# GpSimd in place of ScalarE for the column added onto routed token rows, with a shorter fill in the scatter step

## Chip, cores and metric

One Trainium2 chip, one of its cores. The metric is the device time in microseconds (us) of one execution, and its median over three runs. Engines are named as in the profile: PE (TensorE matmul), PEld (its weight loads), DVE (VectorE), ACT (ScalarE), POOL (GpSimd) and SP (SyncE, which here only starts DMAs).

## What is computed

An input of 32 images, each 128 channels by 56 x 56 pixels, in float32, runs through two layers:

```python
# layer 0
x = x + conv3x3(sign(groupnorm(x)), sign(w)) * Alpha
# layer 1, on tokens: t is (32, 3136, 128)
t = t + q * sum_n(k * v)                  # q, k, v from layernorm(t)
n = layernorm(t)
p = softmax(n @ router_w + router_b)      # 8 experts, the best two per token
top_p, top_i = top_k(p, 2); top_p /= sum(top_p)
t = t + sum_k top_p[k] * (n @ expert_w[top_i[k]] + expert_b[top_i[k]])
```

The last line is the part around the change: each of 3136 tokens per image goes to two of eight experts, and the two results, weighted, are added to the token.

## The kernel before

An image has 25 chunks of tokens, 24 of 128 rows and one of 64; a chunk in SBUF is a tile of 128 partitions (tokens) by 136 columns: 128 channels and 8 columns for the routing. The experts are computed in two ways. For the first chunks of each image, and for all chunks of the last four images, they are **dense**: all eight experts run on every token, and the gates multiply the input (`gated`, L1172, on DVE, then eight expert products on PE, L1190). For the other chunks the tokens are **sorted**. Images 0 to 27 form four groups (8, 8, 7 and 5 images) in which 8, 8, 8 and 12 chunks are dense, so 17 (or 13) chunks per image are sorted, 456 in all. A sorted chunk takes this way:

1. `row_scalars` (DVE, L1371 to L1390) works out per token a column `a` (a layernorm shift) and four scalars, which it writes into columns 128 to 131 of the token's row. `row_numbers` (DVE, L1350 to L1355) works out to which row of a DRAM table `rows` each token goes, by its pair of experts.
2. `row_add` (ACT, L1395) adds `a` onto the 128 channels of the chunk, in place: one activation of 128 x 128 float32 with a bias per partition.
3. `scatter` (POOL, L1402) is an indirect DMA that writes the chunk's 128 rows of 132 columns to their places in `rows`. POOL's share of that work is the profile's DMA_INDIRECT.
4. When all images of a group are scattered, tiles of 128 rows of one pair of experts are loaded from `rows` (`tile_load`, SP), turned (PE, L1735; ACT, L1746), multiplied with the two experts' weights (PE, L1758), scaled and shifted (ACT, L1776 and L1783), summed (DVE, L1788 and L1793) and stored to a DRAM table `res`.
5. `gather` (POOL, L1481), again an indirect DMA, fetches the rows of `res` for a chunk, again 456 in all. They are turned back to channels (`back_turn`, PE, L1501), copied (ACT, L1514) and stored to the output.

Each indirect DMA, scatter or gather, passes through `in_turn` (L1579 to L1587): it waits until the fourth indirect DMA before it has landed, and after it POOL runs a **fill**, a memset of an unused tile `idle` (128 partitions x 480 bytes, L1586), before the next one. The scatter has a `nop` ahead of its DMA.

The order of instructions on every engine is set by a planner, `in_order`, that runs when the kernel is built. Every piece of work is a step with a due time, an engine, an estimated duration and the steps that it waits for (`after`). Rings such as `ROOM["sent"] = 4` limit how far one step may run ahead of another in the plan. Each engine then issues its steps strictly in that order. An image's work is due 60 us after that of the image before, and about three images are in flight (`HELD = 3` buffers of tokens), so that the transposes of image i+3 into the token buffer (`xt`, PE, L677) wait for the scatters of image i. The scatter steps are planned at `SEND = 1.75` us, and so are the gathers; `row_scalars` of image i waits for the last `row_add` of image i-2, since the column `a` has two buffers. For images 0 to 7 POOL also sums one-hot blocks (`hot_blocks`, L1305 and L1307, three adds of 128 x 112 bfloat16), whose result goes by way of PE's `places` and ACT's `count_on` to `row_numbers`.

Of the kernel before, what the change touches and what calls it, by code (L numbers as in the profile page):

```python
# [48 lines left out]
AF = mybir.ActivationFunctionType  # L49
ALU = mybir.AluOpType  # L50
# [4 lines left out]
C = 128  # L55
# [22 lines left out]
}  # L78
ON_POOL = 8
IN_FLIGHT = 4  # L80
SEND = 1.75
HELD, LOADS, LOAD_LANDS = 3, 4, 10.0

GATE_LANDS, SPREAD_LANDS, STORE_LANDS, TILE_LANDS, GATHER_LANDS = 5.0, 6.5, 5.0, 6.0, 12.0
# [3 lines left out]
Q_GROUP = 3  # L88
# [11 lines left out]
BANKS, EMPTIES = ("ps", "acc", "ff"), 7.0  # L100
ROOM = dict(
    ps=5, acc=1, ff=2, y=3, qs=3, tt=4, bc=4, gt=2, gated=2,
    t_in=3, turned=2, v=3, w=2, back=12, sent=4, o=2, late=3,
)


# [82 lines left out]
def conv_attn_moe_kernel(  # L189
# [19 lines left out]
    nc = tc.nc  # L209
# [3 lines left out]
    n_ck = -(-n_tok // C)  # L213

    def rows_of(c):
        return min(C, n_tok - c * C)
# [21 lines left out]
    const = ctx.enter_context(tc.tile_pool(name="const", bufs=1))  # L238
# [241 lines left out]
    def at(due, key, engine, work, do, *args, after=(), take=(), free=(), delay=0.0, slack=0.0):  # L480


        if isinstance(work, float):
            steps[key] = Step(due, key, engine, work, do, args, after, take, free, delay, slack, 0.0)
            return
        running = []

        def go_on():
            if not running:
                running.append(do(*args))  # L490
            next(running[0], None)

        lag = LAG if isinstance(work, list) else 0.0
        for j, w in enumerate(work):
            last = j == len(work) - 1
            part = key if last else (*key, "part", j)
            steps[part] = Step(
                due, part, engine, w, go_on, (), [(*key, "part", j - 1)] if j else after,
                [] if j else take, free if last else [], delay if last else 0.0, slack, lag,
            )  # L500
# [53 lines left out]
    def plan_image(i: int):  # L554
        s = base(i)
        d = {"x": x_all[i % HELD], "tok": tok_all[i % HELD]}
        st1, st2 = st1_all[i % 2], st2_all[i % 2]
        move = move_all[i % 2]
        n_dense = DENSE[group_of[i]] if i in group_of else n_ck
# [56 lines left out]
        for k in range(n_load):  # L616
# [3 lines left out]
                after=[("load", i, k - 1) if k else ("load", i - 1, 1)]  # L620
                + ([("gn_sum", 0, GN_PARTS - 1)] if i == 1 else [])
                + reads_to((k + 1) * n_tok // n_load),
                delay=7.0 if i == 1 else 13.0 if i < HELD else LOAD_LANDS,
            )
        for j in range(GN_PARTS):
# [6 lines left out]
                after=[("gn_neg", i), ("conv", i - 1, min(j + 1, n_conv - 1))],  # L632
# [3 lines left out]
            after=[("gn_sum", i, j) for j in range(GN_PARTS)],  # L636
# [4 lines left out]
            after=[("gn_mean", i), ("gn_sign", i - 2, GN_PARTS - 1)], free=[("ps", ("gn_mean", i))],  # L641
# [64 lines left out]
        for b in range(n_conv):  # L706
            at(
                s + 5.5 * b, ("conv", i, b), "PE", 1.75, conv, b,
                after=[("gn_sign", i, j) for j in range(min(b + 2, GN_PARTS))]
                + [("conv", i, b - 1) if b else ("conv", i - 1, n_conv - 1), ("binary", 2)],  # L710
                take=["ps"],
# [3 lines left out]
                after=[("conv", i, b)], free=[("ps", ("conv", i, b))],  # L715
            )
        for g in range(n_blk):
# [5 lines left out]
                after=[("conv_add", i, b), ("xt", i, g - 1)] + sent_from(i - HELD, g),  # L723
                take=["ps"],
# [3 lines left out]
                after=[("xt", i, g)], free=[("ps", ("xt", i, g))],  # L728
# [3 lines left out]
                after=[("xt_out", i, g), ("var1", i - 2)],  # L732
# [3 lines left out]
            after=[("stats1", i, g) for g in range(n_blk)]  # L736
# [101 lines left out]
        for g in range(n_blk):  # L838
# [3 lines left out]
                after=[("rstd1", i), ("scaled", i, g - 1), ("scaled", i - 1, last_b)], take=["y"],  # L842
# [3 lines left out]
                after=[("scaled", i, g), ("gram", i, g - 1), ("kv_7", i - 1)],  # L846
                take=[] if g else ["acc"], free=[("y", ("scaled", i, g))],
# [3 lines left out]
            after=[("gram", i, last_b), ("kv_8", i - 1)], free=[("acc", ("gram", i, 0))],  # L851
# [10 lines left out]
        for j, engine, work, do, after, take, free in kv_steps:  # L862
            after = [(k, i) for k in after]
# [5 lines left out]
        for g in range(n_blk):  # L869
# [3 lines left out]
                after=[("kv_4", i), ("scaled", i, g), ("stats1", i, g)],  # L873
# [43 lines left out]
        for j, cs in enumerate(q_groups):  # L917
# [4 lines left out]
                after=[("kv_8", i), ("project", i, j - 1)] + biased, take=["ps"],  # L922
# [3 lines left out]
                after=[("project", i, j)], take=["qs"], free=[("ps", ("project", i, j))],  # L926
# [3 lines left out]
                after=[  # L930
                    ("project_out", i, j), ("route_1", i - 2), ("row_scalars", i - 2),
                    ("var2", i - 2),
                ],
                free=[("qs", ("project_out", i, j))],
# [144 lines left out]
        def parts_store():  # L1079
# [16 lines left out]
            after=[("project_add", i, j) for j in range(last_q + 1)]  # L1096
# [12 lines left out]
            after=[("route_5", i), ("gate_turn", i - 1)],  # L1109
# [3 lines left out]
            after=[("dense_gates", i)], take=["ps"],  # L1113
# [3 lines left out]
            after=[("gate_turn", i), ("gate_parts", i - 1), ("parts_store", i - 1)]  # L1117
# [4 lines left out]
            after=[("gate_out", i), ("spread", i - 2, last_units(i - 2))], delay=GATE_LANDS,  # L1122
# [3 lines left out]
            after=[("gate_out", i)], free=[("ps", ("gate_turn", i))],  # L1126
# [3 lines left out]
            after=[("gate_parts", i), ("spread", i - 2, last_units(i - 2))], delay=GATE_LANDS,  # L1130
# [81 lines left out]
        for b in dense_blocks:  # L1212
            share = (cols_of(b)[1] - cols_of(b)[0]) / WIDE
            n = b * pairs
            at(
                begin + n * unit - 4, ("tt_turn", i, b), "PE", 0.45 * share, to_channels, b,
                after=[("project_add", i, c // Q_GROUP) for c in blocks[b]]
                + [("gated", i, n - 2), ("gate_turn", i)]
                + [("tt_turn", i, b - 1) if b else ("tt_turn", i - 1, last_dense(i - 1))],
                take=["ps", "tt"],  # L1220
# [3 lines left out]
                after=[("tt_turn", i, b)], free=[("ps", ("tt_turn", i, b))],  # L1224
            )
            for k in range(pairs):
                n = b * pairs + k
# [3 lines left out]
                    after=[("gate_store", i), ("spread", i, n - 1), ("spread", i - 1, last_unit)]  # L1231
# [6 lines left out]
                    take=[bc_ring] if k else [bc_ring, "gt"], delay=SPREAD_LANDS,  # L1238
# [3 lines left out]
                    after=[("spread", i, n), ("tt_out", i, b)]  # L1242
                    + [("gated", i, n - 1) if n else ("gated", i - 1, last_unit)],
                    take=["gated"], free=[(bc_ring, ("spread", i, n))], slack=0.5,
# [4 lines left out]
                    after=[("gated", i, n), ("experts", i, n - 1)],  # L1249
                    take=[] if k else ["ff"],  # L1250
                    free=[("gated", ("gated", i, n))] + ([] if k else [("gt", ("spread", i, n))]),
# [15 lines left out]
        group = group_of[i]  # L1267
# [124 lines left out]
        def row_add(c):  # L1392
            n = rows_of(c)
            t = d["tok"][:n, c, :C]
            nc.scalar.activation(  # L1395
                t, t, AF.Identity, bias=d["a"][:n, c - n_dense : c - n_dense + 1]
            )

        def scatter(c):
            n = rows_of(c)  # L1400
            nc.gpsimd.nop()
            dma = nc.gpsimd.indirect_dma_start(  # L1402
                out=groups[group]["rows"],
                out_offset=bass.IndirectOffsetOnAxis(
                    ap=d["row_no"][:n, c - n_dense : c - n_dense + 1], axis=0
                ),
                in_=d["tok"][:n, c, :ROW],
                in_offset=None,
            )
            alone(f"rows{group}", dma, in_turn(dma))  # L1410
# [20 lines left out]
        )  # L1431
        at(
            s + 135, ("row_scalars", i), "DVE", [0.37, 0.19, 0.18, 0.31], row_scalars,
            after=[("route_5", i), ("row_add", i - 2, n_ck - 1)],
        )
        for k, c in enumerate(range(n_dense, n_ck)):
            at(
                s + 138 + 2 * k, ("row_add", i, c), "ACT", 0.30, row_add, c,
                after=[("row_scalars", i), ("row_numbers", i), ("project_add", i, c // Q_GROUP)],
                take=["sent"],  # L1440
            )
            at(
                s + 140 + 2 * k, ("scatter", i, c), "POOL", SEND, scatter, c,
                after=[("row_add", i, c), ("row_numbers", i), ("open", group)],
                free=[("sent", ("row_add", i, c))], delay=3.0,
            )
        if first_of_group:
            at(
# [29 lines left out]
        def gather(c):  # L1478
            d["back", c] = bpool.tile([C, C], F32, tag="back", bufs=14, name=f"back_{i}_{c}")
            n = rows_of(c)  # L1480
            dma = nc.gpsimd.indirect_dma_start(  # L1481
                out=d["back", c][:n, :],
                out_offset=None,
                in_=groups[group]["res"][: quads_of(group) * WIDE, :],
                in_offset=bass.IndirectOffsetOnAxis(
                    ap=d["res_no"][:n, c - n_dense : c - n_dense + 1], axis=0
                ),
            )
            in_turn(dma)
            not_single(dma)  # L1490
            d["back_by", c] = dma
            if len(back_read) + 14 > n_gather[0] >= 14 and back_read[n_gather[0] - 14] is not None:
                behind(dma, back_read[n_gather[0] - 14])
            n_gather[0] += 1
# [80 lines left out]
        return m  # L1575

    moved = []
    idle = const.tile([C, 480], mybir.dt.uint8, name="idle")

    def in_turn(dma):  # L1580

        before = moved[-IN_FLIGHT:][:1] if len(moved) >= IN_FLIGHT else []
        for b in before:
            tc.add_manual_dep(dma.ins, b.name, in_turn_dep, reason="few under way")
        moved.append(dma.ins)
        nc.gpsimd.memset(idle, 0)  # L1586
        return before  # L1587

    def tiles_of(g):
        return (group_rows[g] + N_PAIR * (C - 1)) // C  # L1590
# [358 lines left out]
```

## Time and profile before

| what | value |
|---|---|
| median of 3 runs | 2173.2 us (2168.15 to 2180.11) |
| the profiled execution's own time | 2168.68 us |
| its span, first to last instruction | 2167.0 us |
| busy: PE, DVE, POOL, ACT | 2045.6, 1874.1, 1585.2, 1582.2 us |
| scatters on POOL (L1402) | 456, mean 1230 ns |
| gathers on POOL (L1481) | 456, mean 1153 ns |
| fills on POOL (L1586) | 912, mean 515 ns |
| row adds on ACT (L1395) | 456, mean 430 ns in all forms, 176.2 us in sum |

The profile comes from one execution. A row of the groups gives the line, engine and operation, what is written from what, the count, the busy time in us and the mean duration in ns, and behind the last bar how long the engine had been idle just before these instructions and what released it. A busy engine is not always a limit: which one is, is read stage by stage, from the chain of work that ended last and from the waits. "issue" is time in which an engine waited for nothing that the profile shows.

### The profile page before, as it was taken

Reading aid. Unit: us, or ns where it says so; the run is one execution under the profiler, and the core shown is the slowest. Engines: PE = TensorE matmul, PEld = TensorE weight load, DVE = VectorE, ACT = ScalarE, POOL = GpSimd, SP = SyncE. Lnnn points to the kernel's source line nnn. Section 1 sums busy time; section 2 is a strip of 40 time slices with the busy share of each in tenths; the row PEclk is TensorE's granted clock in tenths of the full one; section 3 lists DMA queues with packets and bytes.
Section 4 is the critical chain, followed back from the end, with each engine's and each line's share of the span. In section 5 each row is a group of like instructions: output and inputs, shape, how many; then the busy total and the mean of one; then the engine's idle time right before and its main releaser. Section 6 shows DMA issues by size and latency. Waiting matters only on the chain.

```text
span 2167.0 us, 46389 instructions
## 1 busy us (share of the span) xinstructions
PE 2045.6 (94%) x12224; PEld 1446.1 (67%) x12224; DVE 1874.1 (86%) x5492; ACT 1582.2 (73%) x5136; POOL 1585.2 (73%) x1981
## 2 busy tenths in 40 slices
PE   4989999999999999999999999999999999999889
PEld 2756666666777777657777777667777766676544
DVE  4799999999999999989998899898778988867765
ACT  5767777768888888769988898677887775655311
POOL 3066666765545443888888888888989889999883
PEclk9999999999999999999999999999999999999899
DMA  4144554456555655577775676677786878878787
GB/s 174 31 142 158 188 183 172 150 163 209 180 172 185 186 145 190 183 220 226 237 234 152 196 230 202 206 222 231 228 247 191 254 260 239 280 218 284 231 253 284
DMA packets 327868, 440.49 MB, mean 203 GB/s; under 512 B 61804, under 2 KB 228316, under 8 KB 327612
## 3 DMA queue, kind: packets, MB, share of 16 engines
q1 hardware_dynamic: 296092, 370.92, 54.7%
q0 software_dynamic: 29936, 59.87, 9.1%
q10 hardware_dynamic: 1584, 6.75, 0.8%
q8 instruction: 104, 1.70, 0.3%
q14 instruction: 152, 1.25, 0.2%
HBM read 308.04 MB, written 129.32 MB: 202 GB/s over the span
## 4 chain that ended last, share of the span: by engine, by line
PE 52%; DVE 21%; POOL 8%; DMA 8%; issue 4%; ACT 4%; SPq 2%; DVEq 0%; POOLq 0%; ACTq 0%
PE ff L1190 17%; PE cv L652 8%; PE to L1758 8%; PE gram L763 5%; PE q L885 4%; POOL back L1481 4%; DMA back<-res,res_no 3%; DVE gated L1172 3%; DVE st L692 3%; POOL idle L1586 2%; DVE st L915 2%; PE turn L1735 2%; DVE x L663 2%; DMA bc<-gp 2%; DVE tok L836 2%
## 5 line engine op out<-in xcount | busy, mean ns | idle before, releaser
L1402 POOL DMA_INDIRECT rows<-tok,row_no x456 | 561.0, 1230 | 342.3 <-ACT tok L1395 247.2
L1190 PE MATMUL ff<-gated,ew_d 128*128 128x512 f32 (+1 forms) x1424 | 655.0, 589 | 24.4 <-DVE gated L1172 23.0
L1481 POOL DMA_INDIRECT back<-res,res_no x456 | 525.6, 1153 | 92.1 <-issue 67.0
L1586 POOL MEMSET idle<- 128x480 uint8 x912 | 469.7, 515 | 0.6
L1172 DVE TENSOR_TENSOR gated<-tt,bc 128x1024 f32<-128x1024 f32 (+1 forms) x332 | 391.7, 1185 | 86.6 <-PE ff L1190 41.5
L652 PE MATMUL cv<-xs,w_bin 128*128 128x440 bf16 (+3 forms) x2016 | 424.3, 358 | 6.2 <-ACT xs L609 5.3
L1190 PEld LDWEIGHTS ff<-gated,ew_d 128*128 128x128 f32 x1424 | 254.7, 192 | 238.9 <-issue 188.8
L1776 ACT ACTIVATE v<-to,t_in 128x128 f32<-128x128 f32 x556 | 264.8, 477 | 94.5 <-PE to L1758 68.0
L652 PEld LDWEIGHTS <-w_bin 128*128 128x128 bf16 x2016 | 199.0, 99 | 169.8 <-issue 21.0
L1758 PEld LDWEIGHTS to<-ew_s,turned 128*128 128x128 f32 x2224 | 271.5, 193 | 36.2 <-issue 26.8
L1758 PE MATMUL to<-ew_s,turned 128*128 x2224 | 284.7, 278 | 7.0 <-issue 3.4
L899 ACT ACTIVATE qs<-q,r 128x136 f32<-128x136 f32 (+1 forms) x800 | 246.5, 398 | 44.0 <-PE q L885 32.2
L750 ACT ACTIVATE y<-tok,r 128x128 f32<-128x128 f32 (+1 forms) x800 | 253.1, 406 | 12.1 <-PE gram L763 4.4
L885 PE MATMUL q<-move,x 128*128 128x144 f32 (+1 forms) x1600 | 239.8, 293 | 1.1 <-DVE neg_gm L606 0.6
L763 PEld LDWEIGHTS gram<-y 128*128 128x128 f32 (+1 forms) x1600 | 199.6, 191 | 43.5 <-issue 24.2
L885 PEld LDWEIGHTS q<-move,x 128*128 128x128 f32 (+1 forms) x1600 | 212.3, 191 | 18.8 <-issue 7.8
L763 PE MATMUL gram<-y 128*128 128x129 f32 (+1 forms) x1600 | 215.6, 278 | 2.8 <-ACT y L750 1.9
L1783 ACT ACTIVATE w<-to,t_in 128x128 f32<-128x128 f32 x556 | 215.8, 388 | 0.0
L692 DVE BATCH_NORM_STATS2 st<-tok 128x6 f32<-128x128 f32 (+1 forms) x800 | 185.1, 278 | 18.7 <-ACT tok L683 15.8
L915 DVE BATCH_NORM_STATS2 st<-tok 128x6 f32<-128x128 f32 (+1 forms) x800 | 190.2, 282 | 7.2
L912 DVE TENSOR_TENSOR tok<-tok,qs 128x408 f32<-128x408 f32 (+1 forms) x288 | 155.4, 539 | 34.0 <-ACT tok L904 28.6
L1395 ACT ACTIVATE tok<-tok,a 128x128 f32<-128x128 f32 (+1 forms) x456 | 176.2, 430 | 0.3
(238 smaller groups left out, 2984.0 us busy)
## 6 DMA issues: line engine op xcount, KB each, us to landing
bc<-gp SPq DMA_DIRECT2D x320, 512.0 KB
x<-in_x_dram SPq DMA_DIRECT2D x116, 392.0 KB
t_in<-rows SPq DMA_DIRECT2D x556, 66.0 KB
res<-v SPq DMA_DIRECT2D x139, 256.0 KB
out_dram<-o SPq DMA_DIRECT2D x107, 256.0 KB
out_dram<-tt SPq DMA_DIRECT2D x85, 256.0 KB
x<-gp SPq DMA_DIRECT2D x20, 512.0 KB
rows<-zeros SPq DMA_DIRECT2D x116, 66.0 KB
```

What stands on the lines that cost most here:

```text
L652: nc.tensor.matmul(cv[:, r0:r1, c0:c1], lhsT=w_bin[:, t, :], rhs=xs[:, b * ROWS + dy + r0 : b * ROWS + dy + r1, dx + c0 : dx + c1], start= ...
L692: nc.vector.bn_stats(st[:n, c, :], d["tok"][:n, c, :C])
L750: m = nc.scalar.mul(y[:n, j, :C], d["tok"][:n, c, :C], d["r1"][:n, c : c + 1])
L763: m = nc.tensor.matmul(d["gram"], lhsT=y[:n, j, :C], rhs=y[:n, j, :], start=(c == 0), stop=(c == n_ck - 1),)
L885: nc.tensor.matmul(p[:n, k, :], lhsT=d["x"][:, c * C : c * C + n], rhs=move, start=True, stop=True,)
L1172: nc.vector.tensor_tensor(g[:, :, :n], d["tt", b][:, :n].unsqueeze(1).to_broadcast([C, 2, n]), d.pop(("bc", b, k))[:, :, :n], ALU.mult,)
L1190: nc.tensor.matmul(d["ff", b][:, :n], lhsT=ew_d[:, e * C : (e + 1) * C], rhs=g[:, j, :n], start=False, stop=(e == N_EXP - 1),)
L1402: dma = nc.gpsimd.indirect_dma_start(out=groups[group]["rows"], out_offset=bass.IndirectOffsetOnAxis(ap=d["row_no"][:n, c - n_dense : c - ...
L1481: dma = nc.gpsimd.indirect_dma_start(out=d["back", c][:n, :], out_offset=None, in_=groups[group]["res"][: quads_of(group) * WIDE, :], in_o ...
L1586: nc.gpsimd.memset(idle, 0)
L1758: nc.tensor.matmul(p[:, k, j, :], lhsT=t[:, n * C : (n + 1) * C], rhs=ew_s[:, bass.ds(d["cols", q][j][n], C)], start=True, stop=True,)
L1776: nc.scalar.activation(d["v", q][:, n, :], p[:, k, 0, :], AF.Identity, bias=row[:, C + 2 : C + 3], scale=row[:, C : C + 1],)
```

## The change

The row add moves from ACT to POOL, as a `tensor_scalar` of POOL, and becomes a part of the scatter step: a fill of 192 bytes in place of 480, the row add, the DMA. The `nop` goes. The fill now stands ahead of its DMA, in the gather too, where it stays 480 bytes. The step `row_add` and its ring `sent` leave the plan; what waited for `row_add` waits for `scatter`, and the scatter takes over what `row_add` waited for. The plan's cost of a scatter goes from 1.75 to 1.8.

```diff
-SEND = 1.75
+SEND, SCATTER = 1.75, 1.8
+IDLE = 480
...
         def row_add(c):
             n = rows_of(c)
             t = d["tok"][:n, c, :C]
-            nc.scalar.activation(
-                t, t, AF.Identity, bias=d["a"][:n, c - n_dense : c - n_dense + 1]
+            nc.gpsimd.tensor_scalar(
+                t, t, d["a"][:n, c - n_dense : c - n_dense + 1], None, ALU.add
             )

         def scatter(c):
             n = rows_of(c)
-            nc.gpsimd.nop()
+            apart(192)
+            row_add(c)
             dma = nc.gpsimd.indirect_dma_start(
...
-            after=[("route_5", i), ("row_add", i - 2, n_ck - 1)],
+            after=[("route_5", i), ("scatter", i - 2, n_ck - 1)],
         )
         for k, c in enumerate(range(n_dense, n_ck)):
             at(
-                s + 138 + 2 * k, ("row_add", i, c), "ACT", 0.30, row_add, c,
-                after=[("row_scalars", i), ("row_numbers", i), ("project_add", i, c // Q_GROUP)],
-                take=["sent"],
-            )
-            at(
-                s + 140 + 2 * k, ("scatter", i, c), "POOL", SEND, scatter, c,
-                after=[("row_add", i, c), ("row_numbers", i), ("open", group)],
-                free=[("sent", ("row_add", i, c))], delay=3.0,
+                s + 140 + 2 * k, ("scatter", i, c), "POOL", SCATTER, scatter, c,
+                after=[
+                    ("row_scalars", i), ("row_numbers", i), ("project_add", i, c // Q_GROUP),
+                    ("open", group),
+                ],
+                delay=3.0,
             )
...
         def gather(c):
             d["back", c] = bpool.tile([C, C], F32, tag="back", bufs=14, name=f"back_{i}_{c}")
             n = rows_of(c)
+            apart(IDLE)
             dma = nc.gpsimd.indirect_dma_start(
...
         moved.append(dma.ins)
-        nc.gpsimd.memset(idle, 0)
         return before
+
+    def apart(n):
+        nc.gpsimd.memset(idle[:, :n], 0)
```

More of the change, by code (lines that the diff above doesn't have):

```diff
@@ L102 @@
     ps=5, acc=1, ff=2, y=3, qs=3, tt=4, bc=4, gt=2, gated=2,
-    t_in=3, turned=2, v=3, w=2, back=12, sent=4, o=2, late=3,
+    t_in=3, turned=2, v=3, w=2, back=12, o=2, late=3,
 )
@@ L1577, in conv_attn_moe_kernel @@
     moved = []
-    idle = const.tile([C, 480], mybir.dt.uint8, name="idle")
+    idle = const.tile([C, IDLE], mybir.dt.uint8, name="idle")
     def in_turn(dma):
```

## The prediction, made before the result was known

> **What bounds the kernel now.** I read the page's rows of groups first, then the busy time by stage, the chain of waits by stage, and last the timelines of POOL and DVE around single instructions. The page says that four engines are well filled:
>
> ```profile
> PE 2045.6 (94%) x12224; PEld 1446.1 (67%) x12224; DVE 1874.1 (86%) x5492; ACT 1582.2 (73%) x5136; POOL 1585.2 (73%) x1981
> ...
> L1402 POOL DMA_INDIRECT rows<-tok,row_no x456 | 561.0, 1230 | 342.3 <-ACT tok L1395 247.2
> ...
> L1481 POOL DMA_INDIRECT back<-res,res_no x456 | 525.6, 1153 | 92.1 <-issue 67.0
> L1586 POOL MEMSET idle<- 128x480 uint8 x912 | 469.7, 515 | 0.6
> ...
> L1395 ACT ACTIVATE tok<-tok,a 128x128 f32<-128x128 f32 (+1 forms) x456 | 176.2, 430 | 0.3
> ```
>
> POOL's work is nothing but steps of DMA and fill. POOL waits for the row add 247.2 us, which looks like the prize; when it waits is the question. The busy time of four stretches (columns: PE, PEld, DVE, ACT, POOL with counts, then clock, DMA share, GB/s) answers it:
>
> ```profile
> 200.00:450.00 250.00, 239.19 (x1408) 161.14 (x1407) 243.99 (x802) 181.67 (x608) 162.51 (x189) 1.00 0.46 155
> 500.00:894.00 394.00, 392.02 (x2565) 293.81 (x2564) 366.40 (x1088) 347.81 (x1158) 210.99 (x238) 1.00 0.62 189
> 894.00:1760.00 866.00, 832.22 (x5261) 610.35 (x5260) 766.64 (x2292) 696.24 (x2267) 766.97 (x917) 0.99 0.71 214
> 1760.00:2167.00 407.00, 374.36 (x1823) 241.96 (x1823) 296.79 (x619) 184.23 (x553) 335.34 (x398) 0.96 0.81 259
> ```
>
> Stage A (to 500) is DVE's: 243.99 of 250. Stage B is PE's: 392 of 394. There POOL has spare time, and its long waits for ACT are waits for the next image. From the first gather at 894 (stages C and D) **POOL runs flat out** to its last gather at 2133: each step is 0.16 to 0.17 us of start ("issue"), 1.15 to 1.23 of DMA, 0.515 of fill. Beyond 0.17 per step, its idle time, added up over the trace, is 12.2 us before C's 201 scatters, 11.1 before C's 258 gathers and 7.0 before D's 197: 30 us in 1240. So POOL is a floor under stages C and D. The chain of waits agrees less strongly: in C some 10% of it is POOL's own (scatters 3.0%, gathers 4.2%, fills 3.1%) and 4.4% gather transfers, but PE holds most.
>
> **What a POOL instruction that reads SBUF meets.** The trace has 24 such, the adds of `hot_blocks`. This is one beside DVE:
>
> ```profile
> 148.57 1.31 POOL L1305 TENSOR_TENSOR hot_sum<-hot 128x112 bf16<-128x112 bf16 x1 [1.05 <-DVE gate L1006]
> ```
> ```profile
> 148.42 1.22 DVE L1172 TENSOR_TENSOR gated<-tt,bc 128x1024 f32<-128x1024 f32 x1
> 149.56 0.40 DVE L1017 TENSOR_TENSOR hot<-hot,gate 128x64 f32<-128x64 f32 x1
> 149.88 0.21 DVE L1018 TENSOR_TENSOR hot<-hot,gate 128x64 f32<-128x64 f32 x1
> ```
> ```profile
> L1305 POOL TENSOR_TENSOR hot_sum<-hot x8: 373/374/1311, 106.2 to 439.4; 128x112 bf16<-128x112 bf16 x8
> ```
> ```profile
> L1586 POOL MEMSET idle<- x912: 507/513/557, 116.4 to 2134.0; 128x480 uint8 x183
> ```
>
> (The last two give minimum, median and maximum ns.) The add, 0.374 us alone, lasted until 0.24 us after DVE's `gated`, which has two inputs in SBUF, had ended; then DVE's next such operation took 0.40 in place of 0.21. Each delays the other. The fill, which only writes, never took over 557 ns in 912 times. The scatters themselves read their row numbers from SBUF, and show the same: of 456, 189 began with no two-SBUF-input operation of DVE under way and took 1.009 us on average; 45 began with over 0.8 us of one still to run and took 1.807. DVE is in such an operation at 58% of the scatters' starts.
>
> The Trainium skill says this of the mechanism (SBUF — State Buffer, "Who interferes with whom"): a DVE instruction with two SBUF inputs contends with a GpSimd instruction that reads SBUF, not with one that only writes, and the loser is blocked for the whole instruction. Rows and rule agree on who waits; they differ in size, as DVE lost 0.19 us to an add of 0.374. By the rule, DVE's price below (stage A) would be 17 x 0.5 x 0.29 = 2.5 us per image, 20 over A's eight images, where the row makes it 1.6 and 13.
>
> **The change part by part.**
>
> *POOL's scatter step.* Before: 0.17 + 1.230 + 0.515 = 1.915 us. The `nop` shows no cost: scatters and gathers start alike. What changes:
> - Fill of 480, gone: -0.515.
> - Fill of 192: memsets of 128 elements took 0.195 to 0.206, of 480 took 0.515; between them 0.20 + 64 x 0.315/352 = +0.257.
> - The row add, alone. No such POOL row. Least: the 128x128 float32 memset, 0.206; most: the two-input add's mean, 0.420; nearest: the `affine_select` of 128x128 float32, one read and one write, 0.287. I take 0.29.
> - Its wait for DVE. Least: the mean excess of the 24 adds, (8 x 118 + 16 x 34)/24 = 0.06; most: the scatter DMA's, 1.230 - 0.977 = 0.25. The time still to run in DVE's two-input operations, averaged over stage C, is 0.216. I take 0.20.
> - The DMA now waits for a POOL result. `hot_blocks`' dependent adds stand 0.08 apart; least 0. I take 0.08. Ahead of this, its wait for the fourth DMA before stays; the wait for ACT goes.
>
> Sum: -0.515 + 0.257 + 0.29 + 0.20 + 0.08 = **+0.31 us** per scatter, bounds +0.01 and +0.49. Gathers change nothing: a fill ahead of a DMA instead of behind the one before stands between the same two. Behind a waiting row add stand the next scatters, gathers, and in images 0 to 7 the next `hot_blocks`; for scatters wait the tile loads of the group and the transposes of image i+3. `row_scalars` now waits for POOL two images back instead of ACT; `row_numbers` beside it waited for the same scatter already, so that adds nothing.
>
> *ACT* loses 176.2 us. In A ACT is at 73%, in D at 45%: nothing. In B the chain has 1.0% on row adds, 4 us, and PE is full anyway: -4 to 0. In C ACT is at 80%, and POOL's excess wait of 12.2 us, much of it for row adds, falls away. I count this within C.
>
> *DVE* is delayed by the row adds' reads: about half of them meet a waiting two-input operation (58% of time it is in one), at 0.19 us: 17 x 0.5 x 0.19 = 1.6 us per image. In A, eight images: 13 us if DVE were the whole chain. DVE holds some 43% of A's chain: 6. I take **+8**, bounds 0 and +14. Also there, scatters of 17 x 0.31 = 5.3 us more use up the 4 us that POOL waits before `hot_blocks` (3.9 us in most images), so this chain becomes late by about 1 us; inside the bounds. In B the 11 us vanish in DVE's 28 idle us: **-2** with ACT's gain, bounds -4 and +3.
>
> *Stages C and D.* POOL gets 201 x 0.31 = 62 us more. Its excess idle takes up to 30; the 34 us between the last gather and the end could shrink to about 12 (a gather lands some 6 us after issue, then turn, copy, store), 22 more. So +10 to +62 by the floor; the chain's own scatters, 3.0% of 866 us = 26 us or 22 of 1.19, give only 22 x 0.31 = 7. I take **+30**: in a stretch where POOL's steps follow each other without a break, the floor is nearer than the chain's first order. Bounds: at +0.01 per scatter, and with ACT relieved, -15; at +0.49, 98.
>
> Sum: 8 - 2 + 30 = **+36 us**. On the profiled execution: 2168.7 + 36 = 2204.7. Its time is 4.5 us under the median of the three runs, so against the median 2173.2 + 36 = **2209**.
>
> The plan's order shifts on every engine once the step is gone: PE, DVE, ACT and SP orders part within the first images, and POOL's scatter and gather runs are cut differently from the second group on, though the last 200 steps are gathers in both. That is worth some us either way (the three runs alone spread over 12); I put no sign on it.
>
> **Rivals.**
> 1. *Faster.* The row add costs POOL no more than the fill that it replaces (+0.01 to +0.05 per scatter), because it mostly finds DVE in one-input or short work, as most of the 24 adds did; ACT, relieved of 11% of its work, shortens its 4% of the chain (87 us) by 10, and POOL's waits for ACT go (12). Time: 2173 - 20 = 2153. It decides once the step grows by under 0.1 us. Against it: the scatters' own 0.25 us of waiting, in the same places.
> 2. *No change.* The step grows by 0.1 to 0.15; 201 x 0.125 = 25 us is swallowed by the 30 us of idle time, A's few us stand: 2173 to 2183, say 2176.
> 3. *Much slower.* +0.45 per scatter: POOL +90 after 894, little of it hidden, scatters late enough that the transposes of image i+3 wait on PE in its strict order, and A loses 14: 2173 + 14 + 75 = 2262; with part hidden 2240.
>
> That the add does not move is excluded: 456 `tensor_scalar`s stand in POOL's order ahead of the scatters, none is left on ACT.
>
> **Chances.** Forecast (2184 to 2235) 0.62; rival 1 0.10; rival 2 0.17; rival 3 0.11. A measurement of this kernel can tell about 0.5% (11 us) from no change: faster 0.10, same 0.17, slower 0.73. The range leaves out the faster half of rival 1 and most of rival 3: 2164 to 2242.
>
> **What would show it.** The row add's line on POOL: mean near 0.49 us with a minimum near 0.29, and a maximum over 1.2. The scatter's own mean unchanged at 1.2. DVE's two-input rows longer by some percent, images in A, whose first convolutions stand 47.8 us apart in the trace of before, 1 to 2 us further apart. POOL without a break from about 900, last scatter later than 1756 by 20 to 45 us, and the last 200 gathers taking 370 us as before. Wrong, if the row add's mean is under 0.35, or POOL shows waits in stage C that my floor denies.

## The result, and the profile after

The changed kernel takes **2353.8 us** (2342.2 to 2358.8, 4 runs) against 2176.7 for the one before (4 runs; the three of the table above gave 2173.2): ratio **1.081, 95% interval 1.076 to 1.087**. The forecast of slower was right; its size, +36 us with a range to 2242, was far too small: +177. The profiled execution took 2342.2 us, with a span of 2340.5.

The page of the changed kernel (lines of code are one to four higher than before):

```profile
PE 2097.2 (90%) x12224; PEld 1478.8 (63%) x12224; DVE 1899.1 (81%) x5492; ACT 1456.0 (62%) x4680; POOL 1864.0 (80%) x2437
...
PE 34%; POOL 25%; DVE 7%; DMA 6%; issue 5%; ACT 2%; POOLq 0%; DVEq 0%; SPq 0%; ACTq 0%
...
L1404 POOL DMA_INDIRECT rows<-tok,row_no x456 | 562.0, 1232 | 207.5 <-POOL tok L1396 110.2
...
L1482 POOL DMA_INDIRECT back<-res,res_no x456 | 523.9, 1149 | 88.9 <-issue 69.9
...
L1396 POOL TENSOR_SCALAR tok<-tok,a 128x128 f32<-128x128 f32 (+1 forms) x456 | 405.5, 889 | 56.1 <-DVE a L1378 47.6
```

The same line of the chain before:

```profile
PE 52%; DVE 21%; POOL 8%; DMA 8%; issue 4%; ACT 4%; SPq 2%; DVEq 0%; POOLq 0%; ACTq 0%
```

POOL's busy time grew by 279 us, and its share of the chain from 8% to 25%. DVE's grew by 25. PE ran the same 12224 matmuls in 52 us more: its granted clock, 0.985 over the execution before, is 0.95 now, and 0.93 in the middle stage below. The clock goes down as the loss goes up (0.973 in the run of 2264 us below, 0.941 in that of 2413). The DMA rows are unchanged. The new row is the row add: 889 ns where I had counted on 490. Its minimum, median and maximum:

```profile
L1396 POOL TENSOR_SCALAR tok<-tok,a x456: 606/664/3105, 109.3 to 1922.2; 128x128 f32<-128x128 f32 x143, 64x128 f32<-64x128 f32 x9
```

Even the fastest of 456 took 606 ns. A whole scatter step, on POOL's timeline of the changed kernel (start, duration, instruction, idle time before it):

```profile
1510.00 0.28 POOL L1590 MEMSET idle<- 128x192 uint8 x1
1510.24 0.70 POOL L1396 TENSOR_SCALAR tok<-tok,a 128x128 f32<-128x128 f32 x1
1511.22 1.49 POOL L1404 DMA_INDIRECT rows<-tok,row_no  x1 [0.28 <-ACT r L521]
```

From the end of one indirect DMA to the end of the next, a scatter step after the first gather took 1.934 us before and 2.587 now (means over 201), +0.65; a gather step 1.868 and 1.858 (means over all 456). Ahead of the first gather the median step went from 1.81 to 2.62.

Where the 173.5 us of span went can be read from four marks in the two traces:

| stage | before | after | more |
|---|---|---|---|
| start to first gather | 894 | 942 | 48 |
| first gather to last scatter | 862 | 982 | 120 |
| last scatter to last gather | 378 | 385 | 7 |
| last gather to end | 33 | 32 | -1 |

The busy time of 250 to 450 us, before and then after (columns as in the prediction):

```profile
250.00:450.00 200.00, 191.46 (x1131) 129.14 (x1129) 195.15 (x641) 145.53 (x488) 129.83 (x149) 1.00 0.46 155
```
```profile
250.00:450.00 200.00, 185.83 (x1025) 121.28 (x1024) 182.58 (x594) 116.13 (x392) 160.98 (x208) 0.96 0.47 152
```

There POOL is still idle for 39 of 200 us, and DVE, which was busy for 195 of them, for 183 only. After the first gather (the last two rows of the table together in the second line):

```profile
942.00:1924.00 982.00, 845.28 (x5175) 623.31 (x5173) 760.70 (x2235) 631.95 (x2030) 874.28 (x1114) 0.93 0.63 189
1924.00:2340.00 416.00, 382.10 (x1833) 245.28 (x1831) 300.21 (x624) 184.73 (x555) 341.64 (x401) 0.96 0.79 252
```

In the middle stage PE has 137 us idle in 982 (34 in 862 before), DVE did the same 761 us in more time, and POOL, at 874 busy, was idle beyond its starts (0.28 us behind a row add, 0.165 behind a fill) for only 9. So POOL's steps set the length of this stage, and a slower PE clock cannot have added much to it. PE now waits there for gathers. From the waits of the whole span, before and then after (us in sum, times, longest):

```profile
PE back_ps L1501 <- DMA back<-res,res_no: 28.3, 13, 4.3
```
```profile
PE back_ps L1502 <- DMA back<-res,res_no: 105.2, 31, 13.8
```

So theory 1: **the loss is POOL's longer scatter step**, paid in full wherever POOL has no slack. Rival 1: the row add's reads of SBUF hold up DVE, and that makes the loss. Rival 2: the new order, or the fills' new place, makes it.

### The profile page after: what moved, and what is told of

It is laid out like the page before. It is cut to its first block, busy times and chain, and to the rows that moved or that the text cites. A ratio compares the mean times of both kernels' runs of the same rounds, so it can differ in the third digit from the quotient of the medians.

```text
span 2340.5 us, 46539 instructions
## 1 busy us (share of the span) xinstructions
PE 2097.2 (90%) x12224; PEld 1478.8 (63%) x12224; DVE 1899.1 (81%) x5492; ACT 1456.0 (62%) x4680; POOL 1864.0 (80%) x2437
## 4 chain that ended last, share of the span: by engine, by line
PE 34%; POOL 25%; DVE 7%; DMA 6%; issue 5%; ACT 2%; POOLq 0%; DVEq 0%; SPq 0%; ACTq 0%
PE ff L1191 10%; POOL back L1482 9%; POOL rows L1404 7%; PE to L1761 6%; PE cv L653 6%; POOL idle L1590 6%; DMA back<-res,res_no 5%; POOL tok L1396 4%; PE gram L764 3%; PE q L886 2%; PE turn L1738 1%; PE back_ps L1502 1%; PE xt L678 1%; DVE st L916 1%; DVE gated L1173 1%
## 5 line engine op out<-in xcount | busy, mean ns | idle before, releaser
L1191 PE MATMUL ff<-gated,ew_d 128*128 128x512 f32 (+1 forms) x1424 | 665.4, 597 | 20.0 <-DVE gated L1173 18.4
L1396 POOL TENSOR_SCALAR tok<-tok,a 128x128 f32<-128x128 f32 (+1 forms) x456 | 405.5, 889 | 56.1 <-DVE a L1378 47.6
L653 PE MATMUL cv<-xs,w_bin 128*128 128x440 bf16 (+3 forms) x2016 | 434.2, 363 | 8.8 <-ACT xs L610 8.8
L1590 POOL MEMSET idle<- 128x480 uint8 (+1 forms) x912 | 364.9, 400 | 2.0
L1761 PEld LDWEIGHTS to<-ew_s,turned 128*128 128x128 f32 x2224 | 276.7, 196 | 37.3 <-issue 26.8
L886 PE MATMUL q<-move,x 128*128 128x144 f32 (+1 forms) x1600 | 248.5, 300 | 5.0 <-ACT tok L684 3.5
L886 PEld LDWEIGHTS q<-move,x 128*128 128x128 f32 (+1 forms) x1600 | 221.0, 198 | 27.4 <-issue 11.9
L693 DVE BATCH_NORM_STATS2 st<-tok 128x6 f32<-128x128 f32 (+1 forms) x800 | 183.7, 277 | 53.0 <-ACT tok L684 36.7
L1515 ACT COPY o<-back_ps 128x512 f32<-128x512 f32 (+1 forms) x135 | 69.9, 521 | 245.6 <-PE back_ps L1502 177.0
L664 DVE SCALAR_TENSOR_TENSOR x<-cv,alpha_col,x 128x448 f32<-128x448 f32 x224 | 151.2, 675 | 73.1 <-PE cv L653 63.1
```

Source lines behind the costliest of these rows:

```text
L653: nc.tensor.matmul(cv[:, r0:r1, c0:c1], lhsT=w_bin[:, t, :], rhs=xs[:, b * ROWS + dy + r0 : b * ROWS + dy + r1, dx + c0 : dx + c1], start= ...
L886: nc.tensor.matmul(p[:n, k, :], lhsT=d["x"][:, c * C : c * C + n], rhs=move, start=True, stop=True,)
L1191: nc.tensor.matmul(d["ff", b][:, :n], lhsT=ew_d[:, e * C : (e + 1) * C], rhs=g[:, j, :n], start=False, stop=(e == N_EXP - 1),)
L1396: nc.gpsimd.tensor_scalar(t, t, d["a"][:n, c - n_dense : c - n_dense + 1], None, ALU.add)
L1590: nc.gpsimd.memset(idle[:, :n], 0)
L1761: nc.tensor.matmul(p[:, k, j, :], lhsT=t[:, n * C : (n + 1) * C], rhs=ew_s[:, bass.ds(d["cols", q][j][n], C)], start=True, stop=True,)
```

## The experiments

All times are medians, each ratio against the kernel before run beside it on the same chip.

**The forms by themselves.** 24 POOL instructions were added to the kernel of before, on its tile of zeros, where POOL was idle:

```diff
         nc.gpsimd.memset(zeros, 0.0)
+        f, fc = zeros[:, :C], zeros[:, C : C + 1]
+        for _ in range(4):
+            nc.gpsimd.tensor_scalar(f, f, fc, None, ALU.add)
+        for _ in range(4):
+            nc.gpsimd.tensor_scalar(f[:, :32], f[:, :32], fc, None, ALU.add)
+        for _ in range(4):
+            nc.gpsimd.tensor_scalar(f, f, 0.0, None, ALU.add)
+        for _ in range(4):
+            nc.gpsimd.tensor_tensor(f, f, f, ALU.add)
+        for _ in range(4):
+            nc.gpsimd.tensor_tensor(f, f, fc.to_broadcast([C, C]), ALU.add)
+        for _ in range(4):
+            nc.gpsimd.tensor_copy(f[:, :64], f[:, 64:128])
```

> The kernel of before with 24 extra POOL instructions, four each of six forms on a tile of zeros, in the stretch ahead of the first scatter where POOL has nothing to do (nothing is left out). In the changed kernel the row add took 0.606 us at least and 0.889 on average. Theory 1: that floor is the price of the instruction itself, not of waiting; the column add over 128 columns takes 0.60 to 0.66 here too. What makes it dear is open: if it is the operand read from SBUF per partition, the same add over 32 columns still takes over 0.45 and the add of a constant 0.30; if it is the elements, 32 columns take about 0.25 and the constant 0.60. The two-input adds should take 0.40, as the one of 112 bfloat16 did. Rival: 0.606 was still waiting for DVE, and the column add takes 0.29 here. Time of the kernel: as before, within 1%.

Groups of POOL, this kernel (busy us, mean ns; lines 468 to 478 are the six forms in that order):

```profile
L468 POOL TENSOR_SCALAR zeros<-zeros 128x128 f32<-128x128 f32 x4 | 2.4, 609 | 0.4
L472 POOL TENSOR_SCALAR zeros<-zeros 128x128 f32<-128x128 f32 x4 | 2.1, 530 | 0.3
L474 POOL TENSOR_TENSOR zeros<-zeros 128x128 f32<-128x128 f32 x4 | 1.6, 398 | 0.3
L476 POOL TENSOR_TENSOR zeros<-zeros 128x128 f32<-128x128 f32 x4 | 1.6, 398 | 0.3
L470 POOL TENSOR_SCALAR zeros<-zeros 128x32 f32<-128x32 f32 x4 | 1.5, 363 | 0.4
L478 POOL COPY zeros<-zeros 128x64 f32<-128x64 f32 x4 | 0.9, 236 | 0.2
```

609 ns is the price of the instruction itself: the four took 603 to 620, two of them with no operation of DVE under way. Neither of my two guesses holds alone: from 32 to 128 columns it grows by 246 ns, 2.6 ns per column on some 280 fixed; a constant in place of the column saves 79. The two-input add, also with the column spread over 128 elements, takes a third less. The kernel took 2168.4 us (one run), as before.

**Order, fills and ACT's relief without the row add.**

```diff
-            apart(192)
-            row_add(c)
+            apart(IDLE)
```

> The changed kernel without the row add on any engine, and with the fill of 480 in the scatter step again (the column a is not added). The plan and the order on all engines are those of the changed kernel, the fills stand ahead of their DMAs, ACT is relieved. Theory 1 (POOL's longer step makes the loss): 2150 to 2185, about the time before. Rival 2 (the new order, or the place of the fills, makes it): 2300 or more.

2178.3 us, ratio 1.003 (1.002 to 1.005). Rival 2 is out. It shows more: ACT is 129 us less busy than before (1453.3 against 1582.2), and with POOL's steps as they were the kernel gains nothing by it.

**POOL's time without the reads.**

```diff
-            apart(192)
-            row_add(c)
+            apart(IDLE)
+            apart(IDLE)
+            apart(256)
```

> The changed kernel with the row add replaced by more fill: per scatter step two memsets of 480 and one of 256, some 1.30 us, so that a step takes about the 2.70 us that it takes in the changed kernel, but nothing on POOL reads SBUF for it (the column a is not added). Theory 1 (POOL's time): 2310 to 2370, as the changed kernel. Rival 1 (the reads hold up DVE, and that makes the loss): 2160 to 2210.

2413.4 us, ratio 1.110 (1.107 to 1.114): above the expected span, since three memsets came to more than I meant. The scatter step was 2.90 us, not 2.70. What matters: with no read of SBUF added, and DVE's busy time at 1873.8 as before (1874.1), the loss is there, and larger with the larger step. Rival 1 fails as the main cause.

**The row add as a two-input add.**

```diff
-            nc.gpsimd.tensor_scalar(
-                t, t, d["a"][:n, c - n_dense : c - n_dense + 1], None, ALU.add
-            )
+            nc.gpsimd.tensor_tensor(
+                t, t, d["a"][:n, c - n_dense : c - n_dense + 1].to_broadcast([n, C]), ALU.add
+            )
```

> The changed kernel with the row add as a two-input add of POOL, the column spread over 128 elements by its access pattern, in place of the add with a per-partition operand. On the tile of zeros these took 0.398 and 0.609 us. Theory 1 (POOL's step is the price): 0.21 us less per scatter, 201 x 0.21 = 42 us after the first gather and some 10 to 30 before it: 2275 to 2315. Rival 1 (the reads that hold up DVE are the price; this form reads twice as many elements): no gain or a loss, 2345 or more.

2263.7 us, ratio 1.042 (1.038 to 1.046), 90 us under the changed kernel and better than expected. Group of the row add:

```profile
L1396 POOL TENSOR_TENSOR tok<-tok,a 128x128 f32<-128x128 f32 x428 | 244.6, 572 | 114.3 <-DVE a L1378 99.5 <-ACT count_h L1341 12.8 <-issue 1.9
```

The step after the first gather fell to 2.251 us. And this form reads twice as many elements and delays DVE more, whose busy time rises from 1899.1 to 1937.8 us: it goes the wrong way for rival 1. All of DVE's delay lies in its operations with two inputs in SBUF: their durations add up to 1364 us before, 1388 in the changed kernel, 1430 here, and 1364 in the run without reads. Times follow POOL's step: 1.93 us gives 2173, 2.25 gives 2264, 2.59 gives 2354, 2.90 gives 2413.

**The row add on POOL for images 0 to 14 only** (their scatters all stand ahead of the first gather), on ACT for the rest:

```diff
+EARLY = 15
...
-            apart(192)
-            row_add(c)
+            apart(192 if i < EARLY else IDLE)
+            if i < EARLY:
+                row_add(c)
...
+            if i >= EARLY:
+                at(
+                    s + 138 + 2 * k, ("row_add", i, c), "ACT", 0.30, row_add, c,
+                    after=ready, take=["sent"],
+                )
...
```

> The row add on POOL, with its fill of 192, for images 0 to 14 only (all scatters ahead of the first gather); images 15 to 27 have it on ACT as before, with the fill of 480. It splits the loss of some 177 us. In the changed kernel the first gather began 48 us later than before, and the rest came after it. Theory 1: this kernel loses the 48 alone, 2210 to 2235, though POOL has idle time there. Theory 1 in its plain form, as the prediction had it (POOL's time counts only from the first gather on; DVE loses 6 to 13 us before): 2170 to 2190.

2218.3 us, ratio 1.021 (1.019 to 1.022): +45, as theory 1 expected and not in its plain form. The first gather began at 941 us, and from there on all went as before (860 us to the last scatter, before 862). So a quarter of the loss arises where POOL was idle for long, against the prediction.

**The one-hot block sums off POOL.**

```diff
-ON_POOL = 8
+ON_POOL = 0
```

> The changed kernel with the one-hot block sums of images 0 to 7 on DVE in place of POOL. There images stand 53 us apart in place of 47.7. If the loss before the first gather comes from the block sums, which wait in POOL's queue behind the longer scatter steps and hold up the row numbers, most of 8 x 5 us is won back, less some 7 us of DVE's own work: 2310 to 2335. Rival: DVE held up by the row adds' reads, or the scatters themselves being late: 2345 to 2365.

2326.4 us, ratio 1.071 (1.069 to 1.073), as expected: 27 us of the 177 won back. In the changed kernel the first convolution of image 10 started at 502 us (468 before); here at 471. At the first gather, which began at 922, 20 of the 48 us are won back. What stood in the way shows on POOL's timeline of the changed kernel, then DVE's:

```profile
260.22 0.67 POOL L1396 TENSOR_SCALAR tok<-tok,a 128x128 f32<-128x128 f32 x1
261.18 1.04 POOL L1404 DMA_INDIRECT rows<-tok,row_no  x1 [0.28 <-POOL tok L1396]
262.23 0.28 POOL L1590 MEMSET idle<- 128x192 uint8 x1
262.47 0.61 POOL L1396 TENSOR_SCALAR tok<-tok,a 64x128 f32<-64x128 f32 x1
263.36 0.96 POOL L1404 DMA_INDIRECT rows<-tok,row_no  x1 [0.28 <-DVE x L664]
264.34 0.39 POOL L1306 TENSOR_TENSOR hot_sum<-hot 128x112 bf16<-128x112 bf16 x1
```
```profile
257.54 0.64 DVE L1294 TENSOR_TENSOR hot<-mark,pair_no 128x476 bf16<-128x476 f32 x1
...
262.45 0.66 DVE L664 SCALAR_TENSOR_TENSOR x<-cv,alpha_col,x 128x448 f32<-128x448 f32 x1
266.94 0.65 DVE L1351 TENSOR_TENSOR own<-hot,places 128x476 f32<-128x476 bf16 x1 [3.83 <-ACT count_h L1341]
```

DVE had the one-hot marks ready at 258.2; POOL sums them only at 264.3, behind the last scatters of the image before; the places and counts follow, and DVE stands idle for 3.83 us until `count_h` comes. The same two steps of this image before, on POOL and on DVE:

```profile
248.30 0.37 POOL L1305 TENSOR_TENSOR hot_sum<-hot 128x112 bf16<-128x112 bf16 x1 [3.96 <-DVE hot L1293]
```
```profile
254.73 0.65 DVE L1350 TENSOR_TENSOR own<-hot,places 128x476 f32<-128x476 bf16 x1
```

POOL was done with those scatters 3.96 us ahead of the marks, and DVE did not wait. In the changed kernel DVE waits in this way at images 1, 3, 5 and 7, for 3.6 to 6.6 us.

**Shorter fills in the kernel of before**, 192 and none:

```diff
-    idle = const.tile([C, 480], mybir.dt.uint8, name="idle")
+    idle = const.tile([C, 192], mybir.dt.uint8, name="idle")
```
```diff
-        nc.gpsimd.memset(idle, 0)
```

> The kernel of before with all 912 fills cut from 480 to 192 bytes; the row add stays on ACT. If POOL's steps are the floor from the first gather on, each is some 0.25 us shorter, 657 of them 164 us, of which PE, idle for 34 of 866 and 33 of 407 us there, lets through at most about 60: 2110 to 2150. Rival: the fill is what keeps the indirect DMAs apart for the other traffic, and shorter fills give nothing or lose: 2170 to 2200.

> The kernel of before with no fill at all, the row add on ACT. With the fill at 192 POOL had 139 us of idle time beyond its starts after the first gather, so it is no longer the floor and PE is. Theory 1: little more is to be won, 2110 to 2135. Rival (the fill keeps the indirect DMAs apart for a reason): slower than with 192, 2140 to 2190.

2127.7 us, ratio **0.979** (0.977 to 0.982), and 2130.2 us, ratio **0.980** (0.978 to 0.982). Shorter steps of POOL make the kernel faster, the other side of theory 1, and both beat both kernels. Between first gather and last scatter, with the fill of 192:

```profile
897.00:1730.00 833.00, 813.63 (x5225) 601.10 (x5224) 754.91 (x2267) 688.42 (x2250) 657.85 (x914) 1.00 0.73 219
```

PE is busy for 814 of 833 us, POOL has 100 us idle beyond its starts, and taking the rest of the fill away brings nothing. I read this as PE having become the bound.

**The change without any fill**, with its row add, and with the two-input add from above:

```diff
-            apart(192)
             row_add(c)
...
-            apart(IDLE)
```

> The changed kernel with no fill at all, in scatter or gather; the row add stays on POOL as in the change. With no fill, POOL's flat-out need after the first gather is about 201 x 2.3 + 456 x 1.4 = 1100 us, under the 1187 us that the kernel of before without fill spends there bound by PE. Theory 1 (POOL's time alone makes the loss after the first gather): that loss, some 125 us, goes altogether and only some 25 to 45 us before the first gather stay: 2150 to 2175. Rival 1 (the reads hold up DVE, whatever POOL's idle time): 2200 or more, as 70 us or more of the loss stay against 2130 without fill.

> The same without fill, and the row add on POOL as the two-input add that took 0.398 in place of 0.609. Theory 1: before the first gather another 10 to 20 us go: 2135 to 2160. If ACT's relief of 176 us is worth something once POOL is no longer the floor, this is where it shows: under 2130, the time of the kernel of before without fill.

2210.8 us, ratio 1.017 (1.013 to 1.021): outside what theory 1 expected, and in the span of rival 1. Against the kernel without fill whose row add is on ACT, 35 us are lost ahead of the first gather, as expected, and 58 from there to the last scatter, where none were expected. The two-input add: 2156.5 us, ratio 0.993 (0.991 to 0.995), as expected, but 26 over that same kernel, 24 of them ahead of the first gather (921 against 897 us); it did not come under 2130, so ACT's relief does not show here either. The stage from first gather to last scatter of the first of them says what I had miscounted:

```profile
932.00:1822.00 890.00, 823.08 (x5198) 607.41 (x5199) 763.03 (x2249) 633.30 (x2040) 722.91 (x658) 0.97 0.69 208
```

With the starts added (0.28 us behind a row add, 0.305 behind another indirect DMA), POOL was idle for 33 of these 890 us; the expectation below counts 37. I had set its need against both stages, but the last 200 gathers stand behind the last scatter in POOL's order and lend it nothing: in this stage alone 201 steps of 2.5 us and 256 gathers fill it. To tell that from rival 1, a step of the same length that reads nothing (the edit is against the first of these two kernels):

```diff
-            row_add(c)
+            apart(IDLE)
+            apart(IDLE)
```

> The changed kernel with no fill in the gathers, and in the scatter step two memsets of 480, some 1.05 us, in place of fill and row add (the column a is not added). A scatter step then takes about the 2.5 us of the kernel without fill whose row add is the one of the change (2211 us), but POOL reads nothing for it. Theory 1, mended: between the first gather and the last scatter POOL had only 37 of 890 us idle in that kernel, so it was still the floor there: 2185 to 2225 here too. Rival 1 (the reads hold up DVE): 2130 to 2155.

2200.0 us, ratio 1.015 (1.010 to 1.019); scatter step 2.49 us against 2.51. Theory 1 holds there too. The 11 us between these two kernels bound what the reads' hold on DVE can have cost beyond POOL's own time; the intervals of the two ratios overlap, so that it cost anything is not shown.

## Why the prediction was wrong

- **POOL's scatter step: the failed term.** I took +0.31 us; measured after the first gather +0.65. The row add alone: **0.606 where I took 0.29**, above my upper bound of 0.42. That one term is 0.32 of the 0.34 missing. The others were near (means over the 201 scatters): fill of 192 0.281 (0.257 predicted); wait for DVE 0.825 less 0.606, 0.22 (0.20); start of the DMA, waits included, from 0.228 to 0.305, 0.08 (0.08); the DMA itself from 1.193 to 1.220; and the row add begins 0.04 before the fill ends, which I had not counted. I took the row add from the nearest row by size and operands, `affine_select` of 128 x 128; the form of the instruction decided instead, and the trace of before held no row of that form.
- **"+30 in stages C and D, between the floor and the chain's first order": wrong a second time.** The floor itself, 201 x 0.65 = 131, was paid almost whole: 120 + 7 us. The 255 gather steps between took 11 us less (1.850 to 1.808 us each), which makes the 120. The evidence for a floor was in the prediction (30 us of slack in 1240), and I halved it because PE held most of the chain. In this kernel the chain's first order would have given 22 x 0.65 = 14 us, so it said little about what a uniform slowdown of one of several full engines costs. With the right step and the floor, less the 52 us that I let idle time and tail take up, C and D alone would have come to 80 to 130. The bound that the 34 us behind the last gather would give way did not come true: 32.
- **Stage A, "+8", bounds to 14: failed.** +45 when done alone. The prediction saw that the longer scatters use up the 4 us ahead of `hot_blocks` (3.9 to 4.0 us in three of the eight images, 1.1 and twice 2.3 in three others), and left it at 1 us because of the 0.31; with 17 x 0.8 = 14 us it is the main thing, as taking the sums off POOL gave 31 of 34 us back at image 10. From there to image 14's first scatter nothing was lost (395.0 us before, 393.6 after, which fits the -2 for stage B). The rest of the 48 is image 14's own 17 longer steps, which the first gather follows in POOL's order and for which the prediction has no term: 30.6 us before, 45.8 after. This last reading is from the traces; no run took it away. With the sums off POOL those 17 steps took 45.9 us again, but the stretch from image 10 to them also grew, by 9 us; why is open.
- **DVE's delay** was cheap: busy +25 us in sum over 456 row adds, where half of them at 0.19 us would make 43.
- **ACT's relief worth little by itself:** right; the run without the row add shows no gain.
- **Who waits for whom:** right, now on 456 instructions. Of the row adds, 187 began with no two-SBUF-input operation of DVE under way and took 0.740 us on average; 17 with over 0.8 us of one to run took 1.585. The memsets of 480 in the run without reads did not wait: 0.508 us on average with none under way, 0.509 with over 0.8 us to run. The Trainium skill's rule (SBUF — State Buffer, "Who interferes with whom") agrees with these rows. The prediction held against its size that DVE lost 0.19 us to an add of 0.374; but when DVE's operation began, at 149.56 us, only 0.32 us of that add were left, so this row decides little.
- **Rivals.** The third, +0.45 per scatter with 2240 to 2262, was nearest, and had the scatters' lateness in it; it got 0.11, with my own upper bound at +0.49. It was still 92 us short. Faster and no change, at 0.27 together, did not come.

## What to carry to other kernels

Price an instruction that the trace does not show by its form, and where no row has that form, keep the upper bound well above the nearest row; here adds over 128 columns took 0.40 to 0.61 us by their form. An engine whose idle time, beyond its starts, is some per cent of a stage or less (30 us in 1240 here) is close to a floor: added work there was paid almost in full (127 of 131 us), stage by stage, and work that its order puts in a later stage lends no slack to an earlier one. Where an engine has idle time, look also at who waits for its results: a quarter of the loss arose there. Before moving work onto such an engine, look whether something on it can go: cutting the fill won 2%, where moving the add cost 8%.

## What the runs showed of the hardware

- On POOL an add of a per-partition column over 128 x 128 float32 took 0.609 us, of a constant 0.530, and of a tile to itself, or of the same column spread by a zero step, 0.398. The Trainium skill (GPSIMD Engine Reference, "Engine selection") has two-input work on GpSimd at about half of VectorE's speed and one-input work at roughly line rate. By these rows the one-input `tensor_scalar` is the slower of the two on POOL, and the measurement decides.
- An indirect DMA started 0.28 us behind the row add whose result it moves, 0.16 to 0.17 behind a fill, and 0.305 behind another indirect DMA (medians). So leaving out a fill of 192, which takes 0.274 us, shortens an undisturbed step by some 0.13 only, an estimate from these three numbers.
- Two SBUF inputs on POOL held DVE longer than one: DVE's busy time rose by 64 us with the two-input row add and by 25 with the other, though the kernel with the two-input add was the faster (2263.7 against 2353.8 us).
